# Layernorm's inverse root through logarithm, exponential and a Newton step, with one table for all of ScalarE's functions

## The chip, the core and the metric

The kernel runs on one core of one Trainium2 chip. The metric is the time of one execution on the device, in microseconds (us). The core has five engines that work side by side, each through its own queue in order: TensorE (PE: matrix products, with its weight loads listed apart as PEld), VectorE (DVE), ScalarE (ACT), GpSimd (POOL) and SyncE (SP), which here only issues transfers. An instruction starts when it is at the head of its engine's queue and the semaphores that it waits for have been raised by the others.

## What is computed

A cross attention block in float32. The input x has 16 batch elements of 1024 rows of 512 numbers; the context has 16 times 64 rows; a conditioning vector for each batch element gives a scale and a shift.

```python
EPS = 1e-05
def _ada_ln(x, c, W_ss, b_ss):
    mu = jnp.mean(x, axis=-1, keepdims=True)
    var = jnp.mean((x - mu) ** 2, axis=-1, keepdims=True)
    h = (x - mu) / jnp.sqrt(var + EPS)
    ss = jax.nn.silu(c) @ W_ss + b_ss
    scale, bias = jnp.split(ss, 2, axis=-1)
    return (1.0 + scale)[:, None, :] * h + bias[:, None, :]
...
xq = _ada_ln(x_q, t_vec, Wss_q, bss_q)
xkv = _ada_ln(x_kv, t_vec, Wss_kv, bss_kv)
q = (xq @ Wq + bq).reshape(B, Lq, nh, dh)
kv = (xkv @ Wkv + bkv).reshape(B, Lkv, 2, nh, dh)
...
scores = jnp.einsum('bqhd,bkhd->bhqk', q, k) / jnp.sqrt(jnp.float32(dh))
attn = jax.nn.softmax(scores, axis=-1)
out = jnp.einsum('bhqk,bkhd->bqhd', attn, v).reshape(B, Lq, H)
return x_q + (out @ Wp + bp)
```

There are 16 heads of 32 numbers. What the change touches is the factor 1/sqrt(var + EPS) of every row, and its product with the row's mean.

## The kernel before

The rows of x are handled in 32 blocks of 512 rows (two blocks to a batch element). A block has four tiles of 128 rows, with a row in each of the 128 partitions. The context is normalised for two batch elements at a time (one tile of 128 rows, variable `b` or `kvb`), once in four blocks.

Each block goes through these steps; the names are functions of the kernel:

- `q_stats` (L260): for each of the four tiles BN_STATS and BN_AGGR on DVE (L246, L247), which leave mean and variance in the small tile `mvq` (128 x 4 x 2). `kv_stats` does the same for a context tile (`mvk`).
- `q_scale` and `kv_scale` (L266, L273) call `rstd_of` (L249). It makes a small tile `rstd` with the inverse root of each row and minus mean times that. It has four instructions: Sqrt on ACT (L252), reciprocal on DVE (L253), a product and a change of sign on POOL (L254, L255). For a block of x the operands are 128 x 4, for a context tile 128 x 1.
- `hidden` (L281): on ACT, x times the inverse root plus the second number (L277).
- `turn` and `move`: 32 x 32 transposes on DVE (L414), then 16 transfers issued by SP (L427), so that the features lie in the partitions.
- `queries` (L449): 4 groups of products on PE (L462), each read back by ACT with a bias (L479).
- `scores(i, z)` for both halves z of the keys: 32 x 32 products on PE (L490) into two tiles of a PSUM pool `ps_s` that holds two; for each, DVE takes maxima (L501) and ACT copies the tile to SBUF (L508). The second half needs the pool's tiles again, so it waits for these copies.
- `maxima` (L513, L522) spreads the maxima as `mb`; `subtract` takes them off the scores, on POOL in nearly all blocks (L535, two instructions of 128 x 2048). `weights` is the Exp on ACT (L541), `sums` DVE's sum over keys (L546). `inverse` (L513, L560, L522) spreads one over the sum as `vb`. `divide` multiplies both halves by it, on POOL (L566, two instructions of 128 x 2048).
- `mix` is the product with the values (L586). The output projection is done, in the main loop, as seven half size products (`product`, L715), each taken up by DVE's `added` (L729), with sums of operands on ACT, DVE and POOL beside them.

The order of all of this is written out by hand: a prologue for blocks 0 to 2 (L738 to L870), a loop for i = 3 to 29 (L873), and an end for the last two blocks. Every engine gets its instructions in this order. At the end of one turn of the loop stand, in this order, `inverse(i)`, `added(i - 1, 7)`, `divide(i)`, `q_scale(i + 3)`, and where i is 4, 8, ..., 24, `kv_scale`; then the last `queries` and `product(i - 1, 5)`; the next turn begins with `added(…, 5)` and `scores(i + 1, 0)`. In every fourth turn (i = 3, 7, ..., 27) `keys` and `value_products` of the next context tile lie between `q_scale` and the last product.

So on DVE the instructions of `rstd_of` stand behind the spread `vb` (L522) and one L729, and ahead of the next L729 and the next L501. On POOL they stand behind the two instructions of `divide`.

The ACT functions of the kernel are Sqrt (L252), Exp (L196, L541) and Identity or copies. Sqrt and Exp lie in different tables: each change from one to the other has a load of the table (ACT_TABLE_LOAD) ahead of it.

Of the kernel before, what the change touches and what calls it, by code (L numbers as in the profile page):

```python
# [9 lines left out]
F32 = mybir.dt.float32  # L10
AF = mybir.ActivationFunctionType
ALU = mybir.AluOpType
# [3 lines left out]
P = 128  # L16
EPS = 1e-5
# [3 lines left out]
def cross_attention_block(  # L21
# [42 lines left out]
    nc = tc.nc  # L64
# [24 lines left out]
    small = ctx.enter_context(tc.tile_pool(name="small", bufs=3))  # L89
    ps_s = ctx.enter_context(tc.tile_pool(name="ps_s", bufs=2, space=PSUM))  # L90
    ps_m = ctx.enter_context(tc.tile_pool(name="ps_m", bufs=1, space=PSUM))

    ctx.enter_context(tc.manual_schedule())


    ring = [0, 1, 2, 3]
# [85 lines left out]
    eps_sb = const.tile([P, 1], F32, name="eps_sb")  # L182
# [65 lines left out]

    def rstd_of(mv, n, tag):  # L249

        rstd = small.tile([P, 2, n], F32, tag=f"rstd{tag}", name=f"rstd{tag}")
        nc.scalar.activation(rstd[:, 0, :], mv[:, :, 1], AF.Sqrt, bias=eps_sb)  # L252
        nc.vector.reciprocal(rstd[:, 0, :], rstd[:, 0, :])  # L253
        nc.gpsimd.tensor_tensor(rstd[:, 1, :], mv[:, :, 0], rstd[:, 0, :], ALU.mult)  # L254
        nc.gpsimd.tensor_scalar(rstd[:, 1, :], rstd[:, 1, :], -1.0, None, ALU.mult)  # L255
        return rstd

    q_mv, kv_mv, q_rstd, kv_rstd = {}, {}, {}, {}
# [7 lines left out]
    def q_scale(i):  # L266
        q_rstd[i] = rstd_of(q_mv.pop(i), NT, "q")
# [5 lines left out]
    def kv_scale(b):  # L273
        kv_rstd[b] = rstd_of(kv_mv.pop(b), 1, "k")
# [680 lines left out]
    y, z = NB - 2, NB - 1  # L955
# [91 lines left out]
```

## Time and profile before

| what | value |
|---|---|
| median of three runs | 1093.31 us (1092.76 to 1093.9) |
| the profiled execution, whole | 1091.81 us |
| its span, first to last instruction | 1090.0 us |
| TensorE clock granted | 1.000 |
| PE busy | 1073.0 us, 98% |
| DVE busy | 874.7 us, 80% |
| POOL busy | 661.5 us, 61% |
| ACT busy | 655.7 us, 60% |
| `divide` on POOL (L566) | 62 of 4538 ns |
| `subtract` on POOL (L535) | 58 of 4556 ns |
| Sqrt on ACT (L252), 128x4 | 32 of 297 ns |
| reciprocal on DVE (L253), 128x4 | 32 of 160 ns |
| the two small ones on POOL (L254, L255), 128x4 | 32 of 208 ns, 32 of 223 ns |

The page of a profile gives, for each engine, the time in which it was busy, then groups of equal instructions with their mean duration and the idle time ahead of them. A busy share says little by itself: an engine that is idle may be waiting for the one that sets the end, and one that is 98% busy may be pacing all others. The chain of waits follows the work that ended last back to its start. The view in order of time shows, for a stretch of the span, each instruction's start and duration, and in square brackets the idle time of its engine ahead of it and what ended it.

### The profile page before, as it was taken

The numbers are of one execution on the slowest core, as the hardware profiler recorded it, in microseconds if no ns is written. First come the engines' busy times: TensorE is split into PE (matmuls) and PEld (weight loads), VectorE is DVE, ScalarE is ACT, GpSimd is POOL, SyncE is SP. The second block draws the span as 40 slices with busy tenths as digits, with TensorE's granted clock in tenths as the row PEclk, the third lists the DMA queues.
The fourth block names the chain that finished last, engine by engine and source line by source line (L and its number), as shares of the span: only waits on it lengthen the run. The fifth ranks groups of instructions, "written<-read, shape, count | busy, mean of one in ns | idle before, by whom it ended". The sixth has DMA issues, their size and how long they took to land.

```text
span 1090.0 us, 20329 instructions
## 1 busy us (share of the span) xinstructions
PE 1073.0 (98%) x8290; PEld 612.9 (56%) x8290; DVE 874.7 (80%) x1132; ACT 655.7 (60%) x804; POOL 661.5 (61%) x288
## 2 busy tenths in 40 slices
PE   6999999999999999999999999999999999999998
PEld 4533365555755556655565656556665555655433
DVE  4689578888698886989868889688888888697893
ACT  4666656657367672767736676465766657467430
POOL 0147785766647764666747766566765666748830
PEclk9999999999999999999999999999999999999999
DMA  9733432444234443344343343343342444232402
GB/s 356 230 105 124 147 127 96 145 148 155 88 115 144 142 141 127 117 133 133 137 149 118 127 143 116 129 155 129 129 139 91 143 155 145 89 112 100 138 29 87
DMA packets 80524, 145.36 MB, mean 133 GB/s; under 512 B 10504, under 2 KB 10656, under 8 KB 80432
## 3 DMA queue, kind: packets, MB, share of 16 engines
q1 hardware_dynamic: 80432, 144.07, 39.5%
q8 instruction: 65, 1.06, 0.4%
q14 instruction: 27, 0.22, 0.1%
HBM read 77.97 MB, written 33.55 MB: 102 GB/s over the span
## 4 chain that ended last, share of the span: by engine, by line
PE 92%; DMA 3%; DVE 2%; ACT 1%; SPq 1%; issue 0%; DVEq 0%
PE pq L462 38%; PE pp L715 31%; PE po L586 7%; PE ps L490 6%; PE pp L613 6%; PE pv L350 2%; PE pk L322 2%; DMA wss_kv<-in_L_xcond_Wss_kv_dram 1%; DMA b_p_sb<-in_L_xcond_bp_dram 1%; DVE m L501 1%; DMA x<-in_x_dram 0%; SPq L427 0%; DVE vb L522 0%; DVE l L546 0%; DMA xt<-ht 0%; ACT s L541 0%
## 5 line engine op out<-in xcount | busy, mean ns | idle before, releaser
L462 PE MATMUL pq<-xt,wq 128*128 128x512 f32 x1024 | 465.9, 599 | 0.1
L566 POOL TENSOR_TENSOR s<-s,vb 128x2048 f32<-128x2048 f32 x62 | 280.0, 4538 | 190.8 <-DVE vb L522 184.8
L535 POOL TENSOR_TENSOR s<-s,mb 128x2048 f32<-128x2048 f32 x58 | 262.8, 4556 | 155.0 <-DVE mb L522 153.0
L462 PEld LDWEIGHTS pq<-xt,wq 128*128 128x128 f32 x1024 | 188.1, 190 | 242.6 <-issue 239.0
L508 ACT COPY s<-ps 128x1024 f32<-128x1024 f32 x128 | 129.6, 1012 | 193.9 <-DVE m L501 186.3
L729 DVE TENSOR_TENSOR r<-pp,r 128x512 f32<-128x512 f32 x189 | 126.6, 670 | 68.3 <-PE pp L715 65.5
L479 ACT ACTIVATE qt<-pq,bqs 128x512 f32<-128x512 f32 x128 | 87.6, 686 | 146.9 <-PE pq L462 142.9
L501 DVE TRANSPOSE_TENSOR_REDUCE m<-ps 128x32 f32<-128x1024 f32 x128 | 152.2, 1227 | 24.1 <-PE ps L490 24.1
L546 DVE TRANSPOSE_TENSOR_REDUCE l<-s 128x64 f32<-128x2048 f32 x64 | 146.4, 2302 | 5.5 <-ACT s L541 5.4
L715 PE MATMUL pp<-w_p_sb,ot 128*128 128x256 f32 x648 | 148.7, 379 | 0.0
L541 ACT ACTIVATE s<-s 128x2048 f32<-128x2048 f32 x64 | 122.3, 1910 | 28.8 <-POOL s L535 23.9
L715 PEld LDWEIGHTS pp<-w_p_sb,ot 128*128 128x128 f32 x648 | 123.1, 190 | 28.3 <-issue 6.5
L715 PE MATMUL pp<-WT,ot 128*128 128x256 f32 x432 | 104.9, 386 | 0.0
L715 PE MATMUL pp<-WT,s 128*128 128x256 f32 x432 | 102.8, 381 | 0.0
L715 PEld LDWEIGHTS pp<-WT,s 128*128 128x128 f32 x432 | 81.5, 190 | 32.2 <-issue 20.5
L277 ACT ACTIVATE x<-x,rstdq 128x512 f32<-128x512 f32 x128 | 97.2, 812 | 2.1 <-POOL rstdq L255 2.1
L715 PEld LDWEIGHTS pp<-WT,ot 128*128 128x128 f32 x432 | 79.8, 190 | 32.4 <-DVE r L729 16.8
L246 DVE BATCH_NORM_STATS2 bs<-x 128x6 f32<-128x512 f32 x128 | 84.4, 659 | 2.5 <-DMA x<-in_x_dram 2.5
L414 DVE STREAM_TRANSPOSE ht<-x 128x512 f32<-128x512 f32 x124 | 77.5, 681 | 4.3 <-ACT x L277 2.1
L522 DVE STREAM_TRANSPOSE mb<-m 128x2048 f32<-128x2048 f32 x32 | 74.0, 2312 | 5.7 <-POOL s L566 2.7
L490 PE MATMUL ps<-qt,kt 32*32 32x512 f32 x2048 | 76.6, 600 | 1.8 <-DVE kt L330 0.8
L586 PE MATMUL po<-s,vt 32*32 32x512 f32 x2048 | 76.0, 598 | 1.2 <-ACT qt L479 1.2
(94 smaller groups left out, 902.9 us busy)
## 6 DMA issues: line engine op xcount, KB each, us to landing
x<-in_x_dram SPq DMA_DIRECT2D x32, 1024.0 KB, 5.7
r<-in_x_dram SPq DMA_DIRECT2D x32, 1024.0 KB, 5.5
xt<-ht SPq DMA_DIRECT2D x496, 64.0 KB, 2.0
out_dram<-r SPq DMA_DIRECT2D x54, 512.0 KB, 2.8
out_dram<-r SPq DMA_DIRECT2D x20, 256.0 KB, 2.0
wss_q<-in_L_xcond_Wss_q_dram SPq DMA_DIRECT2D x2, 1024.0 KB, 8.7
ctx<-in_ctx_dram SPq DMA_DIRECT2D x8, 256.0 KB, 5.8
wss_kv<-in_L_xcond_Wss_kv_dram SPq DMA_DIRECT2D x2, 1024.0 KB
```

Of the source, the lines that this page charges most:

```text
L277: nc.scalar.activation(dst, src, AF.Identity, bias=rstd[:, 1, j : j + 1], scale=rstd[:, 0, j : j + 1])
L462: nc.tensor.matmul(pq.rearrange("p (g n) -> p g n", g=4), lhsT=wq_tiles[b][:, c, o * P : (o + 1) * P], rhs=xt[:, :, c, :], start=(c == 0), ...
L490: nc.tensor.matmul(pss[r // 2][32 * c : 32 * c + 32, r % 2, :], lhsT=kt[rows, c, z * HK : (z + 1) * HK], rhs=qt[rows, c, :], start=True, s ...
L501: nc.vector.tensor_reduce(m_tiles[i][:, z, 2 * e : 2 * e + 2, :], pss[e].rearrange("p r (j a) -> p r j a", a=32), AX.X, ALU.max, apply_tra ...
L508: nc.scalar.copy(s_sb[:, 2 * e : 2 * e + 2, :], pss[e])
L535: eng.tensor_tensor(s_tiles[i, z], s_tiles[i, z], mb_tiles[i], ALU.subtract)
L541: nc.scalar.activation(p, p, AF.Exp, scale=SCALE)
L546: nc.vector.tensor_reduce(l_tiles[i][:, z], s_tiles[i, z].rearrange("p r (j a) -> p r j a", a=32), AX.X, ALU.add, apply_transpose=True,)
L566: eng.tensor_tensor(s_tiles[i, z], s_tiles[i, z], vb, ALU.mult)
L586: nc.tensor.matmul(po[c][32 * r : 32 * r + 32, :], lhsT=vt[rows, z, 32 * r : 32 * r + 32], rhs=p[rows, r, :], start=(z == 0), stop=(z == 1),)
L715: nc.tensor.matmul(acc[k][:, t * HO : (t + 1) * HO], lhsT=rows[:, c, t * P : (t + 1) * P], rhs=cols[:, c, :], start=new and t == 0 and c == 0,
L729: nc.vector.tensor_add(r, acc[k].rearrange("p (t h) -> p t h", t=2), r)
```

## The change

`rstd_of` is written anew. ACT takes the logarithm of the variance plus EPS and then the exponential of minus a half of that, which is the inverse root up to the tables' error. Four instructions on DVE make one Newton step of it, y (3 - (var + EPS) y y) / 2, and a fifth gives minus mean times the result. Nothing of it is left on POOL. Ahead of everything a table that holds logarithm, exponential and the simple functions is loaded, and no other load remains in the program.

```diff
@@
     ctx.enter_context(tc.manual_schedule())
+    nc.scalar.preload_act_table_set("natural_log_exp_and_others")
@@
     def rstd_of(mv, n, tag):
         rstd = small.tile([P, 2, n], F32, tag=f"rstd{tag}", name=f"rstd{tag}")
-        nc.scalar.activation(rstd[:, 0, :], mv[:, :, 1], AF.Sqrt, bias=eps_sb)
-        nc.vector.reciprocal(rstd[:, 0, :], rstd[:, 0, :])
-        nc.gpsimd.tensor_tensor(rstd[:, 1, :], mv[:, :, 0], rstd[:, 0, :], ALU.mult)
-        nc.gpsimd.tensor_scalar(rstd[:, 1, :], rstd[:, 1, :], -1.0, None, ALU.mult)
+        y = small.tile([P, 2, n], F32, tag=f"y{tag}", name=f"y{tag}")
+        y, c = y[:, 0, :], y[:, 1, :]
+        mean, var = mv[:, :, 0], mv[:, :, 1]
+        nc.scalar.activation(y, var, AF.Ln, bias=eps_sb)
+        nc.scalar.activation(y, y, AF.Exp, scale=-0.5)
+        nc.vector.tensor_tensor(c, y, y, ALU.mult)
+        nc.vector.scalar_tensor_tensor(c, var, EPS, c, ALU.add, ALU.mult)
+        nc.vector.scalar_tensor_tensor(c, c, -3.0, y, ALU.add, ALU.mult)
+        nc.vector.tensor_scalar(rstd[:, 0, :], c, -0.5, None, ALU.mult)
+        nc.vector.scalar_tensor_tensor(rstd[:, 1, :], c, 0.5, mean, ALU.mult, ALU.mult)
         return rstd
```

## The prediction

> **What bounds the kernel now.** I read the page's busy times and its chain of waits first, then the groups of ACT, one turn of the loop in order of time, the chain of the first 140 us, and last the only place where POOL and DVE work on two-input operations at once.
>
> ```profile
> PE 1073.0 (98%) x8290; PEld 612.9 (56%) x8290; DVE 874.7 (80%) x1132; ACT 655.7 (60%) x804; POOL 661.5 (61%) x288
> ...
> PE 92%; DMA 3%; DVE 2%; ACT 1%; SPq 1%; issue 0%; DVEq 0%
> ```
>
> TensorE carries 92% of the chain. The loop's turns follow at 30.83 us (the same L462 group starts at 171.59, 202.43 and 233.26 us), with PE instructions end to end. A gain on another engine is worth something only where PE waits for it.
>
> ```profile
> L252 ACT ACT_TABLE_LOAD x30 | 38.5, 1283 | 0.5
> L541 ACT ACT_TABLE_LOAD x30 | 38.5, 1283 | 0.5
> ```
>
> These are the loads that go: 77 us, on an engine that is idle for 40% of the span.
>
> One turn, in order of time (start, duration, engine):
>
> ```profile
> 194.40 0.65 DVE L729 TENSOR_TENSOR r<-pp,r 128x512 f32<-128x512 f32 x1
> 194.62 9.05 POOL L566 TENSOR_TENSOR s<-s,vb 128x2048 f32<-128x2048 f32 x2 [6.18 <-DVE vb L522]
> 194.98 0.16 DVE L253 RECIPROCAL rstdq<-rstdq 128x4 f32<-128x4 f32 x1
> 195.06 0.13 DVE L253 RECIPROCAL rstdk<-rstdk 128x1 f32<-128x1 f32 x1
> 196.67 0.69 DVE L729 TENSOR_TENSOR r<-pp,r 128x512 f32<-128x512 f32 x1 [1.49 <-PE pp L715]
> 197.76 2.38 DVE L501 TRANSPOSE_TENSOR_REDUCE m<-ps 128x32 f32<-128x1024 f32 x2 [0.40 <-PE ps L490]
> 199.04 2.15 ACT L508 COPY s<-ps 128x1024 f32<-128x1024 f32 x2 [0.96 <-DVE m L501]
> 201.29 0.23 PEld L490 LDWEIGHTS ps<-qt,kt 32*32 32x32 f32 x32 [0.33 <-ACT s L508]
> ```
>
> DVE has 1.49 + 0.40 us to spare behind the reciprocals. After that everything is just in time: L501 lets the copy go, the copy ends at 201.19, PE's second scores start at 201.29. Also: the slot of `rstd_of` on DVE lies wholly under POOL's two L566, 194.62 to 203.67 us, begun 0.36 us earlier.
>
> The chain of the first 140 us passes through `rstd_of` where PE does wait:
>
> ```profile
> 70.50 1.06 ACT L252
> ...
> 72.19 0.18 DVE rstdq L253
> 72.37 2.28 DVE m L501 x2
> ...
> 76.32 2.15 PE po L586 x40
> ...
> 128.25 0.06 DVE rstdq L253
> ```
>
> And near the end, in narrow windows:
>
> ```profile
> 1023.47 2.52 POOL L288 TENSOR_TENSOR r<-r,b_p_sb 128x512 f32<-128x512 f32 x2
> 1025.56 2.59 DVE L535 TENSOR_TENSOR s<-s,mb 128x2048 f32<-128x2048 f32 x1
> ...
> 1028.28 3.21 POOL L288 TENSOR_TENSOR r<-r,b_p_sb 128x512 f32<-128x512 f32 x1 [2.28 <-DVE s L535]
> ```
>
> The DVE L535, which otherwise takes 2.28 us (median), took 2.59 as it began 0.43 us before POOL's sum ended. The next L535 ran until 1030.35, and the POOL sum that began under it took 3.21 instead of 1.28: 1.93 us lost of the 2.07 left.
>
> **What the Trainium skill says.** "SBUF — State Buffer", SBUF: two separate sides: VectorE and GpSimd share a pair of SBUF ports under an exclusive lock held for a whole instruction; a DVE operation needs it when it has two SBUF inputs (against a GpSimd operation that reads SBUF) or runs in a two-port mode, and the loser blocks. The two stretched records agree (0.31 and 1.93 us). "VectorE: DVE Perf Modes", The perf-mode tier table: fp32 `tensor_scalar` in SBUF runs in the two-port mode; no run here shows it beside POOL. "ScalarE: Activation LUTs", What ACT_TABLE_LOAD costs: 1283 ns and a drain of 1380 for a switch. The trace has the 1283, but the Sqrt at 190.06 follows a load begun at 188.76, so a switch costs the queue 1.30 us here. Its Table sets section: one set holds both exp and ln, so one load is enough.
>
> **The change, part by part.**
>
> *Loads.* 60 x 1.30 = 78 us leave ACT, nearly all under PE's work. In a turn the first Exp starts 1.3 us sooner (the load at 181.88 goes), but its sum on DVE starts at 186.21 behind two L729, and the second Exp waits for POOL's L535 (185.98): nothing. In the prologue the load ahead of the Exp at 56.11 goes, and the second half's subtraction on DVE (58.08) is late next: at most 0.38 us on ACT, 0.08 on DVE's chain. The load at 70.50 hides under statistics that end at 71.50: 0.3 at most.
>
> *ACT's Ln and Exp.* Ln like Sqrt, 0.30; Exp about 0.23 (L196: 223 ns): half a us per call, in the 4.4 us that ACT is idle before 194.95. Nothing.
>
> *POOL's small pair.* 0.43 us a turn goes, while POOL waits 3 to 10 us for `mb`: nothing.
>
> *DVE's five.* None is in the trace. Nearest rows: 158 ns (reciprocal), 182 (BN_AGGR 128x2), and 0.03 to 0.04 between dependent instructions (8.04 to 8.08): 0.19 each in sequence, 0.95 for five, against 0.08 that a reciprocal advances the queue. So +0.9 for a block, +1.7 with a context tile. In the loop the 1.89 us to spare covers both. In the prologue nothing does: `q_scale(3)` +0.64 (statistics 71.50, Ln, Exp, five: L501 at 73.0 instead of 72.28, less the 0.08), `q_scale(4)` with `kv_scale(2)` +0.88 (L626 ends 89.70, ten make 91.5, L501 was at 90.64), `q_scale(5)` +0.88. Sum +2.4 us: the lower bound, without any port wait.
>
> *The port.* Four of the five read two SBUF operands and the other is a `tensor_scalar`. All stand under L566, and the instruction behind, L729, frees L501, the copies and PE. If they wait as L535 did, the first starts when POOL's first L566 ends (199.15). It must finish before the second can start, and by then POOL's second L566 holds the port until about 203.8. The other four end at 204.5, L729 at 205.1, L501 starts there and not at 197.76: 7.35 us. Idle time of DVE in the rest of the turn comes back as PE is then ahead (0.68 at 201.39 and 0.40 at 202.48): about 6.2 net. By kind of turn:
> - 7 with `q_scale` alone: 6.2 each, 43
> - 6 with `context_features` (PE has 0.44 more work, 31.27): 5.8, 35
> - 6 with `kv_scale` (+0.85): 7.1, 43
> - 7 with `keys` and values, where DVE idles 5.4 us: L566 ends 166.54, then 0.75, L330 0.65, L363 0.75, L729 0.65: L501 at 169.4, was 166.93: 2.5, less 1.1: 10
>
> 131 us. Prologue: `q_scale(3)` meets `divide(0)`, to 75.25: +3.8; `q_scale(4)` meets the four L288 (86.73 to 91.7), then nine small ones: +2.8; `q_scale(5)` meets `divide(2)`, 128.39 to 137.4: +9.5. 16 us. Altogether +147 on the profiled execution's 1091.8: 1239. The median is 1.5 higher (1093.3), so 1240.
>
> **Rivals.**
> - A, the forecast: blocked behind both L566. For it, the two stretched records and the two-input forms. Against: no operation of 128x4 was seen blocked. Without the 1.1 given back (turns 7.35, 7, 8.2 and 2.5): 176 us, 1269. If another 1.1 comes back in each turn of the first three kinds and the last costs nothing, 31 us less: 1209.
> - B: the port is handed over once only, and all five pass between POOL's two. L501 at 200.7: 2.9 - 1.1 = 1.8 a turn, 1.4 and 2.7 for the second and third kind, 0 for the fourth: 37, and 11 in the prologue: 1141. Against: 0.03 us between dependent operations is enough for a waiting POOL.
> - C, the other side: so small operations don't wait for the port (POOL takes it in pieces, or they fall between its accesses). The loop's 1.89 us hides them, +2.4 in the prologue remains: 1095.7. It is no change as long as an operation advances by under 0.18 us, slower above: about evenly divided. For it: the slack is real and PE paces the loop.
> - D: the loads' end helps. The prologue's 0.4 and 0.3 with five operations at half their price: at most 1 us gained, 1092.5; over 2.2 would need another chain than the one shown.
> - E: the stretched turns meet further POOL work and give nothing back: above 1272.
>
> **How the numbers follow.** A 0.63, B 0.17, C 0.15, D 0.02, E 0.03. Time of A: 1240. About 0.2% (2.2 us) is what a measurement can tell from no change. Slower: A, B, E and nearly half of C, 0.89. Same: the rest of C and part of D, 0.09. Faster 0.02. The range takes in A with its bounds and B, leaving out 0.2: 1130 to 1272; A's own is 1209 to 1272.
>
> **What would show it.** Right: two-input 128x4 operations on DVE lasting around 4 us, ending with L566; turns of about 37 us; PE idle ahead of L490 with ACT's copy as its releaser, and DVE hardly waiting for PE any more. One load in all. B: only the first of five stretched, turns of 32.6. C: all five under 0.2 us beside L566, turns of 30.83 and the loss before 140 us. Wrong altogether: turns shorter than 30.8.

## The result, and the profile after

The changed kernel takes 1301.63 us (median of four runs, 1300.32 to 1303.24) against 1093.08 us for the kernel before on the same chip: 1.1907 times as long, with an interval from 1.1887 to 1.1928. It is slower, as forecast, but by 208.6 us where 147 were forecast, and above the range that ended at 1272. The profiled execution took 1302.12 us with a span of 1300.3.

In the changed kernel lines below `rstd_of` carry numbers higher by 13: L501 became L514, L566 became L579, L729 became L742, L715 became L728. Its five DVE instructions are L264 to L268, Ln and Exp are L262 and L263.

The busy times, the granted clock in slices and the chain of waits on the page of the kernel after:

```profile
PE 1135.0 (87%) x8290; PEld 643.6 (49%) x8290; DVE 1121.8 (86%) x1292; ACT 581.0 (45%) x784; POOL 644.2 (50%) x208
PEclk9989789889898998998989999899998899988999
DVE 52%; PE 28%; POOL 13%; ACT 3%; DMA 3%; issue 2%; SPq 1%; DVEq 0%; POOLq 0%
```

PE no longer sets the pace: its share of the chain fell from 92% to 28%, and DVE's rose from 2% to 52%. DVE is busy for 247 us more, though it got only 160 small instructions net. PE is busy for 62 us more with the same 8290 products, and its clock is below 90% of full speed in 15 of the 40 slices (mean 0.934, before 1.000): two things that the next views take apart.

The groups of DVE that hold the new instructions (count, total and mean ns of one, then idle time before):

```profile
L265 DVE SCALAR_TENSOR_TENSOR yq<-mvq,yq 128x4 f32<-128x4 f32 x32 | 115.9, 3620 | 1.1
L264 DVE TENSOR_TENSOR yq<-yq 128x4 f32<-128x4 f32 x32 | 113.1, 3533 | 2.4 <-ACT yq L263 2.4
L267 DVE TENSOR_SCALAR rstdq<-yq 128x4 f32<-128x4 f32 x32 | 10.7, 335 | 1.1
L266 DVE SCALAR_TENSOR_TENSOR yq<-yq 128x4 f32<-128x4 f32 x32 | 10.5, 329 | 1.1
L268 DVE SCALAR_TENSOR_TENSOR rstdq<-yq,mvq 128x4 f32<-128x4 f32 x32 | 4.9, 154 | 0.0
```

Five instructions on four numbers a partition should cost about the same. Two of them take over 3.5 us, and their 229 us are nearly all of DVE's extra 247. L265 and L266 have the same form: the place in the sequence decides, not the operation. `q_scale(5)` in the prologue shows it the other way round. There L264 and L265 are over before POOL's `divide` (L579) begins, and it is L266 and L267 that last long:

```profile
135.37 0.16 DVE L265 SCALAR_TENSOR_TENSOR yq<-mvq,yq 128x4 f32<-128x4 f32 x1
135.43 8.95 POOL L579 TENSOR_TENSOR s<-s,vb 128x2048 f32<-128x2048 f32 x2 [6.03 <-DVE yq L264]
135.56 4.38 DVE L266 SCALAR_TENSOR_TENSOR yq<-yq 128x4 f32<-128x4 f32 x1
139.98 4.42 DVE L267 TENSOR_SCALAR rstdq<-yq 128x4 f32<-128x4 f32 x1
```

One turn of the loop in order of time (the counterpart of the turn shown of before) tells why:

```profile
260.45 8.98 POOL L579 TENSOR_TENSOR s<-s,vb 128x2048 f32<-128x2048 f32 x2 [5.73 <-DVE vb L535]
260.81 4.19 DVE L264 TENSOR_TENSOR yq<-yq 128x4 f32<-128x4 f32 x1
...
265.03 4.42 DVE L265 SCALAR_TENSOR_TENSOR yq<-mvq,yq 128x4 f32<-128x4 f32 x1
...
269.49 0.16 DVE L266 SCALAR_TENSOR_TENSOR yq<-yq 128x4 f32<-128x4 f32 x1
...
269.83 0.68 DVE L742 TENSOR_TENSOR r<-pp,r 128x512 f32<-128x512 f32 x1
270.43 2.37 DVE L514 TRANSPOSE_TENSOR_REDUCE m<-ps 128x32 f32<-128x1024 f32 x2
...
270.66 3.75 PE L728 MATMUL pp<-w_p_sb,ot 128*128 128x256 f32 x8 [4.82 <-DVE r L742]
```

POOL's two instructions of `divide` fill 260.45 to 269.43. L264 ends at 265.00, as the first of them does (264.98), L265 at 269.45, with the second. L266 follows at 269.49 and takes 0.16. L742 and L514, queued behind, come 9 us after L264 started, and PE stands for 4.82 us ahead of the product that needs the bank that L742 reads (a bank is the piece of PSUM that one group of products fills).

That product takes 3.75 us; the same eight (L715) took 1.89 in the kernel before:

```profile
199.47 1.89 PE L715 MATMUL pp<-w_p_sb,ot 128*128 128x256 f32 x8
```

The windows of the turn after (length, busy time of PE, PEld, DVE, ACT, POOL, then the granted clock, of which 1.00 is full speed, the DMA share and GB/s):

```profile
266.00:269.00 3.00, 0.00 (x0) 0.00 (x0) 3.00 (x1) 0.00 (x0) 3.00 (x1) 0.82 0.00 0
269.00:270.50 1.50, 0.00 (x0) 0.00 (x0) 1.43 (x6) 0.00 (x0) 0.43 (x1) 0.50 0.00 0
270.50:272.00 1.50, 1.34 (x3) 1.18 (x4) 1.50 (x3) 0.29 (x1) 0.00 (x0) 0.50 0.00 0
272.00:274.50 2.50, 2.50 (x22) 1.50 (x36) 1.43 (x3) 1.73 (x2) 0.00 (x0) 0.50 0.07 29
274.50:276.00 1.50, 1.50 (x33) 0.42 (x29) 0.92 (x2) 0.00 (x0) 0.00 (x0) 0.92 0.78 302
```

PE is idle from 265.8 on, its clock falls to half at 267.9, and it stays there until about 4 us of work are done. The Trainium skill describes this in "TensorE: Matmul & The Clock Gate", Part 1: The HAM clock gate (half rate after at least one idle window of about 3.4 us, full rate after as long a stretch of work, in windows that run on their own). The traces agree on the two rates, but not on the idle time: here the clock fell 2.1 us after the last product. In the loop of this kernel PE waited 26 times for 4.3 to 6.3 us, and each time the clock fell, 2.1 to 5.4 us after PE had stopped, and was full again 3.8 to 5.7 us after it had resumed. In the kernel before no wait of PE in the loop is over 1 us, and its clock stayed at 1.00.

The turns with `keys` and `value_products` lost most against the forecast. One of them, kernel after:

```profile
340.30 4.42 DVE L265 SCALAR_TENSOR_TENSOR yq<-mvq,yq 128x4 f32<-128x4 f32 x1
...
345.11 0.68 DVE L343 TENSOR_TENSOR kt<-pk,bias_t 128x512 f32<-128x512 f32 x1
345.84 5.62 PE L363 MATMUL pv<-w_kv_sb,xk 128*32 128x128 f32 x128 [5.85 <-DVE kt L343]
...
351.54 0.76 DVE L376 TENSOR_TENSOR vt<-pv,b_v_sb 128x256 f32<-128x256 f32 x2 [5.75 <-PE pv L363]
```

And the same stretch of the kernel before, where DVE's idle time (6.41 us here, 5.36 in the turn that the forecast read) was taken for room:

```profile
288.02 0.69 DVE L330 TENSOR_TENSOR kt<-pk,bias_t 128x512 f32<-128x512 f32 x1 [0.39 <-PE pk L322]
291.35 3.70 PE L350 MATMUL pv<-w_kv_sb,xk 128*32 128x128 f32 x128
...
295.12 0.76 DVE L363 TENSOR_TENSOR vt<-pv,b_v_sb 128x256 f32<-128x256 f32 x2 [6.41 <-PE pv L350]
```

The value products `pv` write the PSUM bank that the keys `pk` had, and `kt` (L330, now L343) is what reads it free. Before, `kt` had been done for 2.6 us when PE came to `pv`. Now `kt` stands behind the blocked five, PE waits 5.85 us for it, and then needs 5.62 instead of 3.70 us at the lowered clock.

Where the 208.6 us went, turn by turn. A turn runs from the first maxima (L501, L514) of block i to those of block i + 1. The columns are the change against the kernel before in us, from one profile each (the spans differ by 210.3 us; 1.3 lie in the last turn, which is not in the table); the last three are experiments told below, with the label's number.

| turns of the loop | forecast, each | after, each | after, sum | keys later (e4), sum | PE busy (e9), sum | both (e11), sum |
|---|---|---|---|---|---|---|
| `q_scale` alone, 7 | 6.2 | 6.4 to 7.2 | 49.4 | 50.8 | 44.8 | 42.4 |
| with `context_features`, 6 | 5.8 | 6.2 to 6.6 | 38.3 | 39.6 | 33.1 | 33.2 |
| with `kv_scale`, 6 | 7.1 | 7.6 to 7.9 | 45.8 | 45.8 | 45.8 | 45.9 |
| with keys and values, 7 | 1.4 | 8.0 to 10.8 | 59.3 | 5.9 | 55.8 | 3.0 |
| prologue, up to block 3's first maxima | 16 | | 16.2 | 17.6 | 18.1 | 20.1 |

### The profile page after: what moved, and what is told of

The parts are those of the page before. It is cut to its first block, busy times and chain, and to the rows that moved or that the text cites. A ratio compares the mean times of both kernels' runs of the same rounds, so it can differ in the third digit from the quotient of the medians.

```text
span 1300.3 us, 20354 instructions
## 1 busy us (share of the span) xinstructions
PE 1135.0 (87%) x8290; PEld 643.6 (49%) x8290; DVE 1121.8 (86%) x1292; ACT 581.0 (45%) x784; POOL 644.2 (50%) x208
## 3 DMA queue, kind: packets, MB, share of 16 engines
q1 hardware_dynamic: 80432, 144.07, 33.1%
## 4 chain that ended last, share of the span: by engine, by line
DVE 52%; PE 28%; POOL 13%; ACT 3%; DMA 3%; issue 2%; SPq 1%; DVEq 0%; POOLq 0%
POOL s L548 13%; PE pp L728 9%; DVE yq L265 9%; DVE yq L264 9%; DVE l L559 6%; DVE m L514 5%; DVE vb L535 5%; PE pp L626 5%; PE pq L475 5%; DVE mb L535 5%; PE ps L503 4%; DVE r L742 4%; PE pv L363 3%; ACT s L554 3%; DVE bs L249 2%
## 5 line engine op out<-in xcount | busy, mean ns | idle before, releaser
L579 POOL TENSOR_TENSOR s<-s,vb 128x2048 f32<-128x2048 f32 x62 | 278.6, 4515 | 197.1 <-DVE vb L535 191.0
L728 PE MATMUL pp<-w_p_sb,ot 128*128 128x256 f32 x648 | 179.6, 435 | 95.9 <-DVE r L742 95.9
L728 PEld LDWEIGHTS pp<-w_p_sb,ot 128*128 128x128 f32 x648 | 138.6, 217 | 136.7 <-issue 109.5
L514 DVE TRANSPOSE_TENSOR_REDUCE m<-ps 128x32 f32<-128x1024 f32 x128 | 152.0, 1226 | 24.3 <-PE ps L503 24.3
L742 DVE TENSOR_TENSOR r<-pp,r 128x512 f32<-128x512 f32 x189 | 126.4, 669 | 35.2 <-PE pp L728 32.0
L265 DVE SCALAR_TENSOR_TENSOR yq<-mvq,yq 128x4 f32<-128x4 f32 x32 | 115.9, 3620 | 1.1
L264 DVE TENSOR_TENSOR yq<-yq 128x4 f32<-128x4 f32 x32 | 113.1, 3533 | 2.4 <-ACT yq L263 2.4
L728 PE MATMUL pp<-WT,ot 128*128 128x256 f32 x432 | 104.9, 386 | 0.0
L728 PE MATMUL pp<-WT,s 128*128 128x256 f32 x432 | 102.8, 381 | 0.0
L728 PEld LDWEIGHTS pp<-WT,s 128*128 128x128 f32 x432 | 81.5, 190 | 32.2 <-issue 20.5
L728 PEld LDWEIGHTS pp<-WT,ot 128*128 128x128 f32 x432 | 79.8, 190 | 32.4 <-issue 21.8
L503 PE MATMUL ps<-qt,kt 32*32 32x512 f32 x2048 | 83.8, 656 | 10.7 <-ACT s L521 9.8
```

Of the source, the lines that this page charges most:

```text
L264: nc.vector.tensor_tensor(c, y, y, ALU.mult)
L265: nc.vector.scalar_tensor_tensor(c, var, EPS, c, ALU.add, ALU.mult)
L503: nc.tensor.matmul(pss[r // 2][32 * c : 32 * c + 32, r % 2, :], lhsT=kt[rows, c, z * HK : (z + 1) * HK], rhs=qt[rows, c, :], start=True, s ...
L514: nc.vector.tensor_reduce(m_tiles[i][:, z, 2 * e : 2 * e + 2, :], pss[e].rearrange("p r (j a) -> p r j a", a=32), AX.X, ALU.max, apply_tra ...
L579: eng.tensor_tensor(s_tiles[i, z], s_tiles[i, z], vb, ALU.mult)
L728: nc.tensor.matmul(acc[k][:, t * HO : (t + 1) * HO], lhsT=rows[:, c, t * P : (t + 1) * P], rhs=cols[:, c, :], start=new and t == 0 and c == 0,
```

## The experiments

The theory: DVE's small instructions wait for POOL's `divide`, one for each of its two instructions, and everything else follows from that. Rivals: the cost lies in the five instructions as such (their number and chain), or in what ACT now does. The runs also had to say why the loss was larger than forecast.

**Without the Newton step** (e2). ACT's part of the change alone: Exp writes the inverse root, POOL's pair stays as it was.

```diff
-        nc.scalar.activation(y, y, AF.Exp, scale=-0.5)
-        nc.vector.tensor_tensor(c, y, y, ALU.mult)
...
+        nc.scalar.activation(rstd[:, 0, :], y, AF.Exp, scale=-0.5)
+        nc.gpsimd.tensor_tensor(rstd[:, 1, :], mean, rstd[:, 0, :], ALU.mult)
+        nc.gpsimd.tensor_scalar(rstd[:, 1, :], rstd[:, 1, :], -1.0, None, ALU.mult)
```

> One table, Ln and Exp; the Newton step is left out, Exp writes the inverse root, POOL makes the second number with two instructions as in the kernel before, and DVE's reciprocal is gone. This is the effect of the table loads alone. Port theory: the 78 us of loads lie off the path, so 1091 to 1094 us, at most 0.2% from the kernel before. Rival (ACT's Ln and Exp cost): above 1100 us.

Measured: 1090.70 us (1089.64 to 1093.45, twelve runs), ratio 0.999 with an interval from 0.9981 to 0.9998. Every turn of the loop is as long as before to 0.01 us; 1.8 us came off ahead of block 4. ACT's busy time fell by 75 us and bought that. Of all variants tried only this one is not slower than before, and its gain is smaller than 0.2%.

**The Newton step on POOL** (e1). The five become eight POOL instructions behind `divide`.

```diff
-        nc.vector.tensor_tensor(c, y, y, ALU.mult)
-        nc.vector.scalar_tensor_tensor(c, var, EPS, c, ALU.add, ALU.mult)
...
+        nc.gpsimd.tensor_tensor(c, y, y, ALU.mult)
+        nc.gpsimd.tensor_scalar(v, var, EPS, None, ALU.add)
+        nc.gpsimd.tensor_tensor(c, v, c, ALU.mult)
...
```

> ScalarE's part as in the changed kernel (one table, Ln and Exp), the Newton step and the second number on POOL, in eight instructions behind divide, nothing on DVE. Port theory (the loss is DVE waiting for POOL's port behind divide): 1091 to 1096 us, no DVE instruction of rstd_of left to wait, turns of 30.83 us. Rival (the loss is the longer chain of dependent small instructions, or Ln and Exp on ACT): near 1300 us, since the chain is even longer.

Measured: 1097.73 us (1096.22 to 1098.92), ratio 1.0048, 1.0034 to 1.0062. It is just above what was expected: no turn of the loop from block 4 on changed, and the 4.4 us of the profiled execution were added ahead of block 4, where ACT waits for POOL's last small instruction. So neither the computation nor its chain costs the 208 us; their place on DVE does.

**The same five, elsewhere on DVE** (e3). In the loop `q_scale` and `kv_scale` stand ahead of `inverse(i)`, when POOL is idle as it waits for `vb`; also `q_scale(5)` ahead of `inverse(2)`.

```diff
+        if nxt3:
+            q_scale(i + 3)
+        if kv == 0:
+            kv_scale(kvb)
         inverse(i)
         added(i - 1, 7)
         divide(i)
-        if nxt3:
-            q_scale(i + 3)
...
```

> The changed kernel with the same instructions, but in the loop q_scale and kv_scale (and q_scale(5) in the prologue) stand ahead of inverse, where POOL is idle, rather than behind divide. Port theory: every turn of the loop goes back to 30.83, 31.27 or 38.24 us and only q_scale(3), which still meets divide(0), keeps its 7 to 8 us: 1099 to 1106 us. Rival (five dependent instructions on DVE cost wherever they stand, now on the path to divide): 1290 us or more.

Measured: 1100.04 us (1099.84 to 1100.29), ratio 1.0066, 1.0052 to 1.008. In the trace of this variant:

```profile
199.24 0.14 DVE L264 TENSOR_TENSOR yq<-yq 128x4 f32<-128x4 f32 x1
199.42 0.16 DVE L265 SCALAR_TENSOR_TENSOR yq<-mvq,yq 128x4 f32<-128x4 f32 x1
...
204.11 4.54 POOL L579 TENSOR_TENSOR s<-s,vb 128x2048 f32<-128x2048 f32 x1 [7.63 <-DVE vb L535]
```

The instructions that took 4.19 and 4.42 us take 0.14 and 0.16, and all turns of the loop are as before. Moving them gave back 202 of the 209 us. What is left, 7.5 us between blocks 1 and 2, belongs to `q_scale(3)`, which this variant leaves under `divide(0)`.

**All of them clear of `divide`** (e10): e3, with `q_scale(3)` behind `scores(1, 1)` and ahead of `maxima(1)`.

```diff
-    q_scale(3)
     scores(1, 1)
+    q_scale(3)
     maxima(1)
```

> As the run with q_scale ahead of inverse, and q_scale(3) moved behind the second scores of block 1, so that its DVE instructions come as divide(0) ends. All of the change's instructions are kept, Newton step too. Port theory: the 7.5 us of the prologue go, and what is left is the price of the five small instructions in the prologue, at most 3 us: 1091 to 1096 us, no turn of the loop longer than before. Rival (some loss comes with the change itself wherever it stands): 1098 us or more.

Measured: 1097.32 us (1097.11 to 1098.67), ratio 1.0052, 1.0038 to 1.0066, between the two expectations. `q_scale(3)` takes 0.16 us an instruction now, but the shifted `q_scale(4)` met POOL's four sums of `residual(1)` (L301):

```profile
87.52 4.95 POOL L301 TENSOR_TENSOR r<-r,b_p_sb 128x512 f32<-128x512 f32 x4
...
89.96 1.31 DVE L264 TENSOR_TENSOR yq<-yq 128x4 f32<-128x4 f32 x1 [0.84 <-ACT yq L263]
91.30 1.19 DVE L265 SCALAR_TENSOR_TENSOR yq<-mvq,yq 128x4 f32<-128x4 f32 x1
```

The wait is as long as what is left of POOL's instruction: 1.3 us behind sums of 1.24, where it is 4.2 behind `divide`. What is still lost against the kernel before lies ahead of block 4; no turn of the loop changed.

**Which form waits.** Three variants of the kernel before get small instructions behind the reciprocal (L255), with unused results.

One product of two SBUF operands (e5):

```diff
+        nc.vector.tensor_tensor(j[:, 0, :], mv[:, :, 0], mv[:, :, 1], ALU.mult)
```

> The kernel before with one more DVE instruction behind the reciprocal: a product of two SBUF operands of 128 x 4 (128 x 1), its result unused. Port theory: it waits for the end of POOL's first L566 (about 4.1 us in a turn), once: 1.6 to 2.7 us lost a turn and 3 to 7 in the prologue, 1135 to 1165 us. Rival (it is the chain of dependent instructions that costs): 1093 to 1095 us.

Five reciprocals, each of the result of the one ahead (e6):

```diff
+        nc.vector.reciprocal(j[:, 0, :], rstd[:, 0, :])
...
```

> The kernel before with five more DVE instructions in a dependent chain, each a reciprocal of 128 x 4 (128 x 1) with one SBUF input, results unused. Port theory: none waits for POOL, about 0.19 us each, hidden in the loop's 1.89 us and 2 to 3 us lost in the prologue: 1094 to 1099 us. Rival (any five dependent small instructions cost as the change did): near 1300 us.

One `tensor_scalar` with a single SBUF operand (e7):

```diff
+        nc.vector.tensor_scalar(j[:, 0, :], mv[:, :, 0], -0.5, None, ALU.mult)
```

> The kernel before with one more DVE instruction behind the reciprocal: a tensor_scalar of 128 x 4 (128 x 1) from SBUF to SBUF, its result unused. If its mode takes the shared port like two inputs do: as with one product, 1135 to 1165 us. If only two inputs count: 1093 to 1095 us.

Measured: e5 1159.4 us (ratio 1.0618, 1.0597 to 1.0639); e6 1100.7 (1.0084, 1.0067 to 1.01); e7 1130.96 (1.0358, 1.0337 to 1.0378). The groups of L255, first of e5:

```profile
L255 DVE TENSOR_TENSOR jq<-mvq 128x4 f32<-128x4 f32 x32 | 110.4, 3451 | 0.0
L255 DVE TENSOR_TENSOR jk<-mvk 128x1 f32<-128x1 f32 x8 | 27.0, 3373 | 0.0
```

of e6 (the mean is of the first of its five):

```profile
L255 DVE RECIPROCAL jq<-rstdq 128x4 f32<-128x4 f32 x32 | 5.7, 178 | 1.1
```

and of e7:

```profile
L255 DVE TENSOR_SCALAR jq<-mvq 128x4 f32<-128x4 f32 x32 | 110.8, 3463 | 0.0
L255 DVE TENSOR_SCALAR jk<-mvk 128x1 f32<-128x1 f32 x8 | 1.0, 130 | 0.0
```

Form and place together decide. Five reciprocals under `divide` don't wait and leave the loop's turns alone; one product of two operands waits, and so does the `tensor_scalar`, for which nothing of before had shown it. That agrees with what the prediction takes from the Trainium skill ("SBUF — State Buffer", SBUF: two separate sides, and "VectorE: DVE Perf Modes", The perf-mode tier table): two SBUF inputs, or one in the two-port mode. A wait for another engine's result is no rival: the product of e5 and the `tensor_scalar` of e7 read only `mvq`, which DVE itself has written, and nothing reads their results. The 128x1 `tensor_scalar` goes through in 0.13 us, six of its eight times while POOL's second L568 (the `divide` of before) runs; in e5 the 128x1 product waits 4.45 us in the same place. No run here shows why. That is why e7 missed its expectation by 4 us: a turn with `kv_scale` lost 2.1 us there, and 6.4 in e5, where two instructions wait, one for each half of `divide`. e6 came 1.7 us above its range. Of its 8.6 us, the profiled execution (1095.98) shows 4.2, all ahead of block 4; the other runs took 1099.8 to 1101.7 at granted clocks of 0.994 to 0.995, and why is open.

**The keys' bank** (e4). The changed kernel with `keys` behind the last `queries`, so that `pv` does not take the bank that `kt` has to free.

```diff
-        if kv == 3:
-            keys(kvb)
         queries(i + 1, 3)
+        if kv == 3:
+            keys(kvb)
```

> The changed kernel with keys behind queries(i + 1, 3) in the seven turns with a context tile, so that the value products take the PSUM bank of the queries and not the bank of the keys, which DVE's L343 sets free. Bank theory (the 8 us of these turns are PE waiting for L343, which stands behind the blocked instructions): they lose 3 to 4 us instead of 8, 1262 to 1280 us in all. Rival (these turns are late as the others are, through L742 and L514): 1298 to 1306 us, unchanged.

Measured: 1252.42 us (1251.5 to 1253.35), ratio 1.146, 1.144 to 1.1481. In its trace, with L264 and L265 blocked as in the kernel after:

```profile
332.06 3.94 PE L363 MATMUL pv<-w_kv_sb,xk 128*32 128x128 f32 x128
332.47 4.47 DVE L265 SCALAR_TENSOR_TENSOR yq<-mvq,yq 128x4 f32<-128x4 f32 x1
...
337.32 0.68 DVE L343 TENSOR_TENSOR kt<-pk,bias_t 128x512 f32<-128x512 f32 x1
337.92 0.75 DVE L376 TENSOR_TENSOR vt<-pv,b_v_sb 128x256 f32<-128x256 f32 x2
```

PE makes `pv` while DVE is blocked, `vt` follows `kt` at once, and these turns lose 0.6 us instead of 8 (the first of them 2.1). 49 us came back, more than the expectation allowed. They hold a share of the clock too, as `pv` takes 3.94 us here and 5.62 in the kernel after.

**The clock** (e8, e9). The changed kernel with four products of 128x512, results unused, ahead of `product(i - 2, 3)`, where PE waits for L742: in every turn after the first (e8), or only where `i % 4` is not 0 (e9), since in the turns behind keys and values PE does not wait there.

```diff
+    def idle_products(i):
+        pi = bank(f"pi_{i}", ring[0])
+        for c in range(NC):
+            nc.tensor.matmul(pi, lhsT=w_p_sb[:, c, :P], rhs=w_q_sb[:, c, :], start=(c == 0), stop=(c == NC - 1))
...
             product(i - 2, 4)
+            if i % 4:
+                idle_products(i)
```

> The changed kernel with four products of 128 x 512 (3.4 us of PE) put between product(i - 2, 4) and product(i - 2, 3), their results unused, so that PE is not idle while DVE is blocked. Clock theory (the turns gave back less than 1.1 us because PE's clock fell to half in the wait and the next products took twice as long): 1.1 to 1.7 us come back in each of 19 turns, 1268 to 1284 us, and the granted clock is above 0.97. Rival (the clock doesn't matter, DVE sets the turn): 1298 to 1306 us.

> The changed kernel with the four products of 128 x 512 (results unused) only in the turns whose start PE waits for DVE, that is not in turns 4, 8, ..., 28, where they were a plain addition of 3.4 us. Clock theory (PE's clock falls in the wait, and the product behind it takes twice as long): 0.6 to 1.0 us come back in each turn with the products, 1282 to 1290 us. Rival (the clock of the products behind the wait doesn't set the turn): 1299 to 1304 us.

Measured: e8 1313.34 us (1313.29 to 1313.39), ratio 1.2028, 1.2004 to 1.2052, outside both ranges. In the turns i = 4, 8, ..., 28 the added work lengthened each by 3.4 us, as PE has no idle time there, while most of the others without `kv_scale` got shorter, by 0.5 to 1.3. e9: 1288.93 us (1288.54 to 1289.32), ratio 1.1805, 1.1783 to 1.1826, as expected. One turn of e9, in order of time (its lines are 11 higher again):

```profile
267.55 3.60 PE L497 MATMUL pi<-w_q_sb,w_p_sb 128*128 128x512 f32 x8
...
272.13 1.96 PE L739 MATMUL pp<-w_p_sb,ot 128*128 128x256 f32 x8 [0.98 <-DVE r L753]
```

With 3.6 us of work put into its wait, PE does the product behind it in 1.96 us instead of 3.75. More work made the kernel 12.7 us shorter: about that much at least was the clock. The turns with `kv_scale` gained nothing.

**Both** (e11): e4 and e9 in one kernel.

> The changed kernel with both edits: keys behind queries(i + 1, 3), and the four products (results unused) in the turns other than 4, 8, ..., 28. If the bank of the keys and PE's clock are what the forecast's sum left out, the two gains add up (49 and 13 us measured apart, less where the first has already taken away a wait), and the time comes to the forecast's 1240: 1236 to 1246 us. If they share a cause, about 1250 us.

Measured: 1236.9 us (1235.62 to 1238.17), ratio 1.1331, 1.1298 to 1.1364. That is within 3.1 us of the forecast's 1240. By the table the first three kinds of turn are within 0.6 us a turn of their forecasts, the turns with keys lost 7 us less in all and the prologue 4 more. So the bank and the clock account for most of what the forecast's sum had left out, but that it then fits within 3 us is in part luck, as these differences cancel.

## Why the prediction was right and where it failed

- *Loads, Ln and Exp, POOL's pair: nothing.* Right: e2, without the DVE part, gives 0.999 of the time before. The bound "at most 1 us gained" was a little low: e2, which drops the reciprocal too, gained 1.8 in the prologue.
- *Small instructions, 0.19 each when they don't wait.* Right: in e3 ten of them, five for a block and five for a context tile, advance the queue by 1.44 us (199.24 to 200.68). The forecast had about 1.7.
- *Waits for both halves of `divide`* (case A). Right, in mechanism and size: medians of 4.19 and 4.42 us, with three short ones behind. Case B, one hand-over, is excluded by this; e7, where just one instruction waits, shows what it would have cost: 1.35 us in a turn with `q_scale` alone (1.5 to 2.9 in e5), forecast 1.8. Case C, no wait, holds for the reciprocals of e6 and not for these forms.
- *Prologue 16 us.* 16.2, by another split: `q_scale(4)` met nothing (POOL's L301 had ended at 94.4, the five began at 96.23), and `q_scale(3)`, forecast at 3.8, brought most of the 7.0 by which block 2 was late. PE's products behind that wait ran at half clock, so its price was larger than the wait.
- *"7 with `keys` and values, where DVE idles 5.4 us: ... 2.5, less 1.1: 10".* This is the step that failed. It measured 59.3 for the seven, 8.0 to 10.8 each where 1.4 were forecast. The working took DVE's idle time there as room into which the late work could move: 0.75 for the last four of the five, then `kt`, `vt` and L729 one behind the other. But that idle time was a wait for PE's `pv`, and `pv` waits for `kt`. The late `kt` moved the whole of `pv` behind it (PE waits 5.85 us for it), and the room was gone. e4, which cuts that dependence alone, gave 49.2 back.
- *"Idle time of DVE in the rest of the turn comes back as PE is then ahead ... about 6.2 net".* A term mis-sized: with `q_scale` alone 6.4 to 7.2 of the 7.35 stayed. PE was not ahead: it had stopped behind the product at 265.8, its clock fell, and the next one took 1.9 us longer. With PE kept at work and keys moved (e11) these turns lose 5.9 to 6.4.
- *The range.* Its upper end took A "without the 1.1 given back" and left the keys turns at 2.5 each, so that an error in that one row could not be inside it. The time fell where case E had it, "above 1272", but not for E's reason, "further POOL work".
- *What would show it.* The stretched two-input instructions and turns of about 37 us (38.0 with `q_scale` alone) came out. PE's idle time was foretold ahead of the scores with ACT's copy as releaser; the larger part stands ahead of L728 with L742 as its releaser (95.9 us in 19 waits).

The sum: 208.6 us more. The keys' bank is 49.2 of it (e4), the clock 12.7 (e9), and both at once 64.7 (e11), 2.8 more than the two apart. These are differences of medians from different chips, on which the kernel before took 1091.6 to 1093.1 us, so each is good to some 2 us. The remaining 144 are DVE's waits and what they hold up. In e11's profile the clock is at 1.00 from 160 us to the last product, so of the 124.5 us still lost in its loop only the 3.5 of the first turn can have to do with the clock; in its prologue, which is now 20 longer, the clock is at 0.89 between 40 and 160 us, and what that costs was not tried.

## What to carry to other kernels

Price a small instruction by its form and by what GpSimd does at that moment: 0.15 us of DVE work cost 4.2 to 4.4 us each under a long GpSimd instruction, once for each such instruction, and no turn of the loop grew where they stood in a place in which GpSimd was idle (e3). Then follow everything queued behind the blocked engine, and count the PSUM banks that it reads free: idle time that is a wait for another engine is no room, if that engine waits for the late one. TensorE paid for its long waits a second time, in the work after them, as its clock had fallen.

## What the runs showed of the hardware that was not expected

- `tensor_scalar` in SBUF waits for GpSimd at 128x4 (4.13 us at 205.98 in e7) but not at 128x1 (0.13 us on average, six of the eight beside a running L568), while a product of two operands waits at both sizes (4.12 and 4.45 us in one turn of e5).
- TensorE's clock fell 2.1 to 5.4 us after its work had ended, in each of the loop's 26 waits of 4.3 to 6.3 us, and eight products took 3.75 instead of 1.89 us. Its busy time rose by 62 us with the same instructions. In e9 waits of 2.5 us brought the clock down four times out of five.
